# Second layer of a two-layer decoder: own scores on four row strips, one set of eight PSUM banks in turn, and a new table of times

## The chip, the core and the metric

The kernel runs on one core of a Trainium2 chip. The metric is device time in microseconds (us) of one execution: the kernel before has a median of 1911.66 us over three runs (1910.52, 1911.66, 1919.04). One execution was also taken with the hardware profiler; its own time was 1925.23 us, and all views of the trace are from that one.

Engines: TensorE (PE, with its weight loads shown apart as PEld), VectorE (DVE), ScalarE (ACT), GpSimd (POOL) and SyncE (SP, which issues DMAs). Matrix products land in PSUM, which has eight banks of 2 KB per partition, that is 512 float32 each.

## The reference

64 sequences of 64 tokens with 128 features go through two decoder layers. The change concerns the second one alone:

```python
x = x + _L1_attn_ref(_layernorm(x), ...)                  # causal, 16 heads of 8
x = x + _L1_xattn_ref(_layernorm(x), ctx_1024, mask, ...) # 16 heads of 64, relative bias
x = x + _L1_ffn_ref(_layernorm(x), ...)                   # top 1 of 8 experts
...
def _L1_attn_ref(x, Wq, bq, Wk, bk, Wv, bv, Wo, bo):
    q = split_heads(x @ Wq + bq)      # 16 heads of 8
    k = split_heads(x @ Wk + bk)
    v = split_heads(x @ Wv + bv)
    att = jnp.einsum('bhqd,bhkd->bhqk', q, k) * scale
    att = jnp.where(mask, att, -jnp.inf)
    att = softmax(att)
    y = jnp.einsum('bhqk,bhkd->bhqd', att, v)
    return y @ Wo + bo
```

The heads of the first attention ("own" attention here) are eight features wide. The cross attention has 64 features to a head and takes its keys and values from `ctx_1024`. The third part weighs the product of one expert out of eight by its probability. The first layer (a linear attention with its experts, a cross attention, and a routed network of experts whose rows are written to and gathered from device memory) is left as it is.

## The kernel before

**Tiles and groups.** Two sequences make a tile of 128 tokens on the 128 partitions; four tiles (`TG`) make a group, and there are eight groups (`NG`). `xres[g]` holds a group's activations for the whole kernel.

**Stages.** The program runs the first layer's three parts one after another, each with its own division of the PSUM banks, and then the second layer as one stage in which all eight groups are in flight, each some way behind the one before. In the trace the second layer's first matmul stands at about 1305 us and the end at 1923.5.

**PSUM.** `psum_pool` (line 135) fixes how many banks each tag has; `psum` (141) hands out the next bank of a tag. In the second layer the line is

```python
psum_pool(pc, "psC", mm=2, sc=2, tp=1, av=2, py=1)     # 1221
```

Projections, biases and logits (`aq`, `ak`, `av`, `apo`, `xqT`, `xkT`, `xv`, `el`, `eb` by the trace's names) take "mm", some of the own queries and keys "sc"; own scores `asc` and cross scores `xsc` take both "sc" banks; every transpose (`pt_...`) and the experts' choice `oht` the one "tp" bank; the sums of the cross attention `xav` and the experts' products `ey` the two "av" banks; the own sums `apy` and the cross output `xz` the one "py" bank. A tile of a tag waits until all readers of the tile that had the bank before are done.

**Pieces and order.** The work of a group is cut into pieces, each a small function that issues a few instructions on several engines:

- `fetch` (two indirect gathers on GpSimd of the first layer's routed rows), `combine` (their weighted addition on VectorE, with the sums of the norm), `norm_root`, `norm_shift`, `norm_rows`, `by_feature` (four transposes and a copy);
- `attn_queries`, `attn_keys`, `attn_masked`, `attn_v`, then for each of four values `attn_scores`, `attn_exp`, two `attn_keys_first` (transposes) and `attn_sums`, then `attn_out_features`, `attn_out`; `attn_keys` and `attn_masked` write the keys into `kx`, which is one buffer, with zeros where another head's features stand, so that 32 rows of keys serve four heads of eight;
- `cross_load` (SyncE loads the group's context), `project`, `cross_v`, and for each of the four tiles `cross_scores`, `cross_exp`, `cross_whole`, two `cross_keys`, `cross_sums`, `cross_out`;
- `ffn_sums`, `ffn_logits`, `ffn_choice`, `ffn_shares`, `ffn_bias`, and `ffn_experts` with `ffn_add` for each tile and each half of the experts (four additions of 128x128 per call on VectorE). The last one stores the group.

A table (from line 1636) gives each piece a time. `at` collects the pieces, `run_todo` issues them sorted by time, and `keep_in_program_order` keeps each engine to that order: the table is the queue of every engine. Times of the first two parts of the table are relative to a group (`when + 4 * g`), so one unit is a quarter of a group's period; the pieces of the first groups and of the last have rows of their own, with absolute times.

**The own scores.** `attn_scores(s, j)` is called four times for a group. Call `j = (ip, rp)` takes two tiles of tokens (`2*ip + i2`) and half of the heads: two of the four strips of 32 rows of TensorE's array (`2*rp + r`). Each strip has a bank for itself, `[P, 2, 4, S]`, filled for two tiles `i2` and both sequences `b` of a tile:

```python
mm(psc[r][S * b : S * b + S, i2],
   lhsT=s.aq[rs, n * S : (n + 1) * S],        # 32 rows x 64 columns
   rhs=s.kx[rs, :, n * S : (n + 1) * S], ...) # 32 x 256
```

Eight such matmuls make a call. `soft_shift` then adds the causal mask `caus` to each bank in one VectorE instruction over 128x512 (result `p_a`, six buffers of the tag "p" shared with `p_x`), and `soft_max` takes the maximum on VectorE and subtracts it on GpSimd. `attn_exp` works on ScalarE, `attn_keys_first` transposes with TensorE and copies with ScalarE, and `attn_sums` multiplies with the values `vz` (16 small matmuls), takes reciprocals of the sums and multiplies by them into `ay`.

Since `mm`, `transpose` and the engines' methods are wrapped, all instructions of the second layer appear in the trace under the wrapper's line: L64 for matmuls and weight loads, L67 for transposes, L80 for VectorE, ScalarE and GpSimd. They are told apart by the names of their tiles.

## Time and profile before

| | us |
|---|---|
| median of three runs | 1911.66 |
| the profiled execution | 1925.23 |
| its span in the trace | 1923.5 |
| TensorE busy in the span | 1833.8 |
| VectorE busy | 1224.6 |
| ScalarE busy | 959.2 |
| GpSimd busy | 586.4 |
| mean granted clock of TensorE | 0.976 |

The span goes from the first to the last recorded instruction. Busy is the time in which an engine had an instruction in work, without register, branch and DMA-issuing instructions. The profile's page cuts the span into 40 slices of 48 us; the rows for TensorE, VectorE and the clock read as tenths:

```profile
PE   8999999997999999999999998998999999999998
...
DVE  5566666636675766666556754554587687676678
...
PEclk9799999998999999999999998998899999999999
```

The second layer begins in the 28th digit. In the views by instruction, a row has the line, the engine, the operation, the result and its sources by their names in the program, their shapes and the number; then the busy time in all and the mean in nanoseconds of one; then the time that the engine was idle just before such instructions and what released it. In the table of waits a row names who waited, on what, and then the sum, the number and the longest wait in us. In the timeline a row has the start and the length of a run of equal instructions.

### The profile page before, as it was taken

How to read it: one execution, taken by the hardware profiler on the slowest of the kernel's cores; microseconds unless marked ns; L12 is line 12 of the kernel's file. 1: busy time of each engine (PE TensorE's matmuls, PEld its weight loads, DVE VectorE, ACT ScalarE, POOL GpSimd, SP SyncE). 2: the span in 40 equal slices, each digit the busy share in tenths (PEclk: the TensorE clock that was granted, in tenths of full speed). 3: DMA queues.
4: the chain of work that ended last, by engine and by line, in shares of the span. 5: the costliest groups of instructions: out<-in, count | busy, mean ns of one | idle time of the engine just before them, and what ended most of it. 6: DMA issues, size and time to landing. Idle time of an engine off the chain costs nothing.

```text
span 1923.5 us, 42409 instructions
## 1 busy us (share of the span) xinstructions
PE 1833.8 (95%) x17390; PEld 1378.1 (72%) x17390; DVE 1224.6 (64%) x3492; ACT 959.2 (50%) x1743; POOL 586.4 (30%) x600
## 2 busy tenths in 40 slices
PE   8999999997999999999999998998999999999998
PEld 6666667676877777777878775774777776777775
DVE  5566666636675766666556754554587687676678
ACT  2444444444554454445454432335577666666553
POOL 1111111102234242423223231006575554543332
PEclk9799999998999999999999998998899999999999
DMA  8000000000000000000000002321000100100000
GB/s 284 16 2 2 1 2 2 2 1 17 7 6 12 6 12 9 9 12 6 6 2 4 1 3 83 109 62 33 20 13 13 18 16 16 17 9 8 8 2 18
DMA packets 39791, 41.67 MB, mean 22 GB/s; under 512 B 4501, under 2 KB 31445, under 8 KB 39340
## 3 DMA queue, kind: packets, MB, share of 16 engines
q1 hardware_dynamic: 29100, 27.40, 4.6%
q0 software_dynamic: 4096, 6.83, 1.6%
q10 hardware_dynamic: 6400, 4.72, 0.8%
q8 instruction: 137, 2.24, 0.5%
q14 instruction: 58, 0.48, 0.1%
HBM read 28.97 MB, written 11.53 MB: 21 GB/s over the span
## 4 chain that ended last, share of the span: by engine, by line
PE 78%; DVE 11%; issue 4%; POOL 2%; ACT 2%; DMA 1%; ACTq 0%; SPq 0%; POOLq 0%; DVEq 0%
PE sc L64 6%; PE pz L64 6%; PE pu L64 5%; PE xq L64 5%; PE down L64 5%; PE ph L64 5%; PE py L64 3%; PE xqT L64 3%; PE pt_p L67 2%; DVE x L80 2%; PE xz L64 2%; PE sp L64 2%; PE ey L64 2%; PE gg_s L64 2%; PE gu_s L64 2%
## 5 line engine op out<-in xcount | busy, mean ns | idle before, releaser
L983 POOL TENSOR_TENSOR p<-p,rc 128x512 f32<-128x512 f32 x128 | 133.2, 1044 | 297.2 <-DVE rc L982 100.2
L64 PEld LDWEIGHTS down<-w2T,hid 128*128 128x128 f32 x1024 | 129.5, 191 | 44.9 <-DVE x L80 21.6
L960 ACT COPY qx<-xq 128x512 f32<-128x512 f32 x128 | 74.6, 583 | 159.1 <-PE xq L64 158.7
L80 ACT ACTIVATE hid<-ph,wa 128x512 f32<-128x512 f32 x128 | 85.7, 686 | 135.3 <-PE ph L64 135.0
L64 PE MATMUL down<-w2T,hid 128*128 128x128 f32 x1024 | 139.7, 279 | 2.5 <-DVE x L80 2.0
L64 PE MATMUL pu<-pT,kvN 128*128 128x512 f32 x256 | 131.8, 598 | 6.3 <-ACT pT L990 6.2
L64 PE MATMUL sc<-kvT,qx 128*128 128x128 f32 x1024 | 136.4, 276 | 0.0
L64 PE MATMUL ph<-hT,w1T 128*128 128x512 f32 x256 | 133.1, 618 | 0.1
L64 PE MATMUL xq<-kvT,wqk 128*128 128x256 f32 x512 | 132.6, 384 | 0.6
L64 PEld LDWEIGHTS sc<-kvT,qx 128*128 128x128 f32 x1024 | 125.4, 192 | 4.5 <-issue 2.6
L64 PEld LDWEIGHTS pz<-wvo,uT 128*128 128x128 f32 x1024 | 118.4, 192 | 9.1 <-issue 6.2
L64 PEld LDWEIGHTS xq<-kvT,wqk 128*128 128x128 f32 x512 | 93.4, 193 | 37.0 <-issue 25.8
L64 PE MATMUL pz<-wvo,uT 128*128 128x128 f32 x1024 | 119.5, 275 | 0.0
L976 DVE TENSOR_REDUCE nmx<-sc 128x4 f32<-128x512 f32 x128 | 88.0, 687 | 48.9 <-PE sc L64 47.9
L1323 POOL DMA_INDIRECT yk<-y_dram,gidx x64 | 65.3, 1021 | 150.6 <-DMA y_dram<-ye 134.3
L990 ACT COPY pT<-pt_p 128x512 f32<-128x512 f32 x128 | 74.2, 580 | 69.5 <-PE pt_p L67 68.7
L979 ACT ACTIVATE p<-p 128x512 f32<-128x512 f32 x128 | 80.7, 631 | 45.8 <-DVE p L978 33.9
L1097 POOL DMA_INDIRECT xg_dram<-xf,sidx x64 | 63.7, 995 | 121.0 <-DVE si L1090 47.5
L80 POOL TENSOR_TENSOR p_x<-p_x,nmx_x 128x512 f32<-128x512 f32 x64 | 65.4, 1043 | 99.9 <-DVE nmx_x L80 96.9
L80 DVE SCALAR_TENSOR_TENSOR x<-ey,oh_e,x 128x128 f32<-128x128 f32 x256 | 88.8, 348 | 9.4 <-PE ey L64 2.1
L1017 DVE TENSOR_TENSOR x<-pz,x 128x128 f32<-128x128 f32 x32 | 9.3, 292 | 132.8 <-PE pz L64 132.8
L981 DVE TENSOR_REDUCE rc<-p 128x4 f32<-128x512 f32 x128 | 87.0, 680 | 8.7 <-ACT p L979 6.4
(327 smaller groups left out, 4255.0 us busy)
## 6 DMA issues: line engine op xcount, KB each, us to landing
xg_dram<-zero SPq DMA_DIRECT2D x10, 256.0 KB, 7.1
xe<-xg_dram SPq DMA_DIRECT2D x8, 320.0 KB, 3.7
y_dram<-ye ACTq DMA_DIRECT2D x8, 320.0 KB, 3.8
x<-in_x SPq DMA_DIRECT2D x8, 256.0 KB, 12.1
cg<-in_ctx SPq DMA_DIRECT2D x8, 256.0 KB, 2.8
rg<-in_rg SPq DMA_DIRECT2D x8, 256.0 KB, 2.8
rd<-in_rd SPq DMA_DIRECT2D x8, 256.0 KB, 3.2
ru<-in_ru ACTq DMA_DIRECT2D x8, 256.0 KB, 2.7
```

The lines of the kernel that those rows point to most:

```text
L64: return in_order(nc.tensor.matmul(*args, **kwargs))
L67: return in_order(nc.tensor.transpose(*args))
L80: return lambda *args, **kwargs: in_order(getattr(self.engine, name)(*args, **kwargs))
L960: nc.scalar.copy(s.qx[hg][:, :, h : h + 2, :].rearrange("p b h q -> p h b q"), pq)
L976: nc.vector.tensor_reduce(out=nmx, in_=psc, axis=AX, op=ALU.max, negate=True)
L979: nc.scalar.activation(pr, pr, AF.Exp, scale=0.125)
L981: nc.vector.tensor_reduce(out=rc, in_=pr, axis=AX, op=ALU.add)
L983: nc.gpsimd.tensor_tensor(out=pr, in0=pr, in1=bcast(rc, P), op=ALU.mult)
L990: nc.scalar.copy(s.pT[hf], pt)
L1017: nc.vector.tensor_tensor(out=xt, in0=pz, in1=xt, op=ALU.add)
L1097: nc.gpsimd.indirect_dma_start(out=xg_dram[:, :], out_offset=bass.IndirectOffsetOnAxis(ap=sidx[:, TG * s.g + i, k : k + 1], axis=0), in_=s ...
L1323: nc.gpsimd.indirect_dma_start(out=yk, out_offset=None, in_=y_dram[:, :], in_offset=bass.IndirectOffsetOnAxis(ap=gidx[:, TG * s.g + i, k : ...
```

## The change

**Banks.** The second layer's five tags become one, "bank", with eight banks that are handed out in turn: the ninth tile in the program's order takes the bank of the first, whatever both are. All `psum("mm" ...)`, `"sc"`, `"tp"`, `"av"` and `"py"` of the stage become `psum("bank" ...)`, and `attn_queries` and `attn_keys` lose the argument that named their tag.

**Own scores.** `attn_scores(s, i)` is still called four times for a group; call `i` now takes one tile of tokens `i` with both of its sequences and all four strips of 32 rows, each strip with its own bank `[P, 4, S]` (half of a bank is filled). The number of matmuls and their shapes stay: eight of 32x64 weights and 256 columns. The mask is added in four instructions over 128x256, two into each `p` tile. `attn_sums(s, i)` takes both `p` tiles of the call, again with 16 matmuls, and ends in one product over 128x128 where there were two over 128x64. Per call the numbers of instructions on TensorE, ScalarE, GpSimd and SyncE stay; VectorE has one more.

**Times.** Every row of the table has a new time. Part of the group's own-attention rows, and of the start:

```diff
-        psum_pool(pc, "psC", mm=2, sc=2, tp=1, av=2, py=1)
+        psum_pool(pc, "psC", turns=True, bank=8)
...
-        caus = mid(cst[:, C_CAUS : C_CAUS + S], 8)
+        caus = mid(cst[:, C_CAUS : C_CAUS + S], 4)
...
     def transpose4(src, nm):
-        pt = psum("tp" if "tp" in banks else "mm", [P, TG, P], f"pt_{nm}")[:, 0:n]
+        pt = psum(next(t for t in ("tp", "bank", "mm") if t in banks), [P, TG, P], f"pt_{nm}")[:, 0:n]
...
-        def attn_scores(s, j):
-            ip, rp = j // 2, j % 2
-            psc = [psum("sc", [P, 2, 4, S], f"asc_{s.g}_{ip}_{rp}_{r}") for r in range(2)]
-            for i2 in range(2):
+        def attn_scores(s, i):
+            psc = [psum("bank", [P, 4, S], f"asc_{s.g}_{i}_{r}") for r in range(4)]
+            for b in range(2):
+                n = 2 * i + b
+                for r in range(4):
+                    rs = slice(32 * r, 32 * r + 32)
+                    mm(
+                        psc[r][S * b : S * b + S],
+                        lhsT=s.aq[rs, n * S : (n + 1) * S],
+                        rhs=s.kx[rs, :, n * S : (n + 1) * S],
...
-            for r in range(2):
-                s.apr[j, r] = soft_shift(
...
+            for rp in range(2):
+                pr = wk.tile([P, 8, S], F32, tag="p", name=f"p_a{s.g}_{i}_{rp}", bufs=6)
+                for r in range(2):
+                    V.tensor_tensor(out=pr[:, 4 * r : 4 * r + 4, :], in0=psc[2 * rp + r], in1=caus, op=ALU.add)
+                s.apr[i, rp] = pr
...
-            py = psum("py", [P, 2, 4, 2, 9], f"apy_{s.g}_{j}")
+            py = psum("bank", [P, 8, 2, 9], f"apy_{s.g}_{i}")
...
-            (-11.4, 5, 7, fetch, 0),
+            (-12.88, 5, 7, fetch, 0),
...
-            (-10.71, 4, 7, combine, 1),
+            (-10.47, 4, 7, combine, 1),
...
-            (-7.7, 3, 7, cross_load),
+            (-7.1, 3, 7, cross_load),
...
-            (-5.45, 3, 7, attn_scores, 0),
-            (-5.09, 3, 7, attn_v),
-            (-5.06, 3, 7, attn_scores, 1),
+            (-6.14, 3, 7, attn_scores, 0),
+            (-5.84, 3, 7, attn_v),
+            (-4.7, 3, 7, attn_scores, 1),
...
-            (-3.94, 2, 7, attn_scores, 2),
+            (-3.91, 2, 7, attn_scores, 2),
...
-            (0.24, 1, 6, cross_scores, 0),
+            (0.18, 1, 6, cross_scores, 0),
...
-            (1.14, 1, 6, cross_sums, 0),
+            (2.49, 1, 6, cross_sums, 0),
...
-            (6.28, 0, 5, ffn_experts, 0, 0),
-            (6.46, 0, 5, ffn_experts, 0, 1),
-            (6.52, 0, 5, ffn_add, 0, 0),
+            (5.98, 0, 5, ffn_experts, 0, 0),
+            (6.04, 0, 5, ffn_experts, 0, 1),
+            (6.19, 0, 5, ffn_add, 0, 0),
```

The pieces themselves, other than the two shown, do the same work as before. The absolute rows of the start now run from 1.444 to 4.58 (before: 1.046 to 5.455), those of the end from 25.005 to 28.11 (before: 25.8 to 27.638).

## The prediction

> **What bounds the kernel now.** I read the page's totals first, then the windows of the second layer (from 1305 us on, the only part that the diff touches), then who TensorE waited for there, and last the timelines of single calls.

> ```profile
> PE 1833.8 (95%) x17390; PEld 1378.1 (72%) x17390; DVE 1224.6 (64%) x3492; ACT 959.2 (50%) x1743; POOL 586.4 (30%) x600
> ```
> ```profile
> 1305.00:1400.00 95.00, 81.49 (x856) 55.96 (x856) 50.38 (x133) 54.25 (x101) 58.44 (x62) 0.84 0.10 27
> 1400.00:1900.00 500.00, 487.05 (x7132) 364.48 (x7122) 368.99 (x1013) 318.29 (x610) 241.25 (x236) 1.00 0.06 12
> 1900.00:1923.50 23.50, 15.96 (x115) 7.98 (x114) 17.49 (x74) 3.38 (x11) 0.55 (x1) 0.86 0.08 23
> ```
> Columns: the stretch, then busy us of PE, PEld, DVE, ACT, POOL, then the granted clock. TensorE is the bound: in the 500 us in the middle it is idle for 12.9 us, while VectorE is busy for 74%, ScalarE for 64%, GpSimd for 48%. So an instruction less on TensorE is worth its time there, and work on VectorE is hidden while its queue is not late. In the first 95 us TensorE is idle for 13.5 us and its clock is 0.84, which costs about 0.16 x 95 = 15 us more.

> ```profile
> PE xav L64 <- DVE x L80: 7.5, 6, 1.4
> PE apy L64 <- DVE ay L80: 2.5, 2, 1.4
> PE xkT L64 <- DVE x L80: 1.6, 6, 0.3
> PE apy L64 <- DVE x L80: 1.4, 3, 0.5
> PE xkT L64 <- ACT v L80: 1.3, 1, 1.3
> PE ey L64 <- DVE x L80: 1.3, 2, 0.9
> PE pt_a L67 <- ACT pT_a L80: 1.1, 1, 1.1
> ```
> These are waits of TensorE for a PSUM bank: each names the reader of the tile that had the bank before (xav and ey share two "av" banks, apy and xz one "py" bank, all transposes one "tp" bank). They are 16.7 us; four smaller ones of the same sort (0.7, 0.7, 0.7, 0.4) make it 19.2 of the 29.3 us of waits in that table.

> **Part 1: own scores on four strips.** One call is 8 matmuls, two rows each in the trace:
> ```profile
> 1510.31 1.09 PE L64 MATMUL asc<-kx,aqT 32*64 32x256 f32 x16
> 1511.33 1.11 PE L64 MATMUL apy<-vz,pT_a 128*64 128x18 f32 x32
> ...
> 239.51 0.69 PE L64 MATMUL sc<-qxa,phi 32*64 32x128 f32 x32
> 240.14 1.05 PE L64 MATMUL down<-w2T,hid 128*128 128x128 f32 x7
> ```
> The first pair is the call on two strips: 1.02 us to the start of the next piece. The second pair is the first layer's scores, which already run on four strips with the same 32 rows by 64 columns of weights: 32 x 128 = 4,096 columns streamed, as many as 16 x 256 here, in 0.63 us. There are 32 calls (8 groups x 4), and the change keeps that number and that of their matmuls. So 32 x (1.02 - 0.63) = 12.5 us go, a little more at half clock: I take -13. Bounds: 0 if the four strips brought nothing, -14 if all were like the fastest.

> **Part 2: more instructions on VectorE.** 64 additions over 128x512 at 685 ns become 128 over 128x256; the first layer has that shape:
> ```profile
> L80 DVE SCALAR_TENSOR_TENSOR x<-ey,oh_e,x 128x128 f32<-128x128 f32 x256 | 88.8, 348 | 9.4 <-PE ey L64 2.1
> L80 DVE TENSOR_TENSOR p_a<-asc,cst 128x512 f32<-128x512 f32 x64 | 41.1, 685 | 22.4 <-PE asc L64 22.2
> L80 DVE TENSOR_TENSOR ay<-apy,arc 128x64 f32<-128x64 f32 x64 | 11.4, 220 | 1.1
> L80 DVE TENSOR_TENSOR sT<-sc,upto 128x256 f32<-128x256 f32 x128 | 45.4, 417 | 14.6 <-PE sc L64 14.5
> ```
> 128 x 417 - 64 x 685 ns = +9.5 us. The 64 products ay of 220 ns become 32 over 128x128, bounded by 220 and 440 ns; the 348 ns of an operation on that shape is near, so 11.1 against 14.1 us, -3. Together +6.5 us on an engine with 131 us idle in the middle: hidden. On a path it shows as latency: the call's scores are read 4 x 0.42 = 1.67 us after the start of the adds, not 1.37. In the first two groups, where TensorE waits for softmax (2.5 us in all for p_a), I take +1; bounds 0 and 8 calls x 0.3 = +2.4.

> [...]

> **Part 3: eight banks in turn.** A tile now waits for the reader of the tile eight before, whatever its kind. I laid each matmul group's undisturbed time from the timelines along TensorE's order in both programs, and took the TensorE work between the last matmul into a bank and the next tile in it. Under 1.05 us it is 85 times of 732 before and 3 of 796 after; under 2 us 211 and 28. The tile before xav in its bank was an expert product whose four additions (4 x 0.35 = 1.4 us) came late:
> ```profile
> 1592.13 0.33 PE L64 MATMUL xav<-pT_x,v 64*64 64x64 f32 x2
> 1593.88 1.16 PE L64 MATMUL xav<-pT_x,v 64*64 64x64 f32 x62 [1.43 <-DVE x L80]
> ```
> At best all 19.2 us go. New short distances: in each of six groups own-score call 2 is followed by two transposes (0.94) and a cross-scores call (1.09), then xav takes the first of its banks, 2.03 us later. Its additions begin 0.1 us after the scores where VectorE is free and, in the trace's first call of a group, 1.30 us after: 1.30 + 1.67 = 2.97, so up to 0.94 us x 6 = 5.6 us come back. Taken at their word the two give -13.6. I take half, -7, since TensorE freed of one wait runs into the next producer sooner: own scores have 9.6 us of TensorE work before their transposes (median) where they had 14.2, cross scores 19 where they had 13. Bounds -19 and +6.

> **Part 4: the new table.** It moves every piece, GpSimd's gathers and SyncE's context loads among them. Gathers were issued ahead of their addition by 0.57 to 1.53 units of time and now by 0.72 to 1.81; a unit is a quarter of a group's period, some 18 us, so the shortest lead is 13 us where it was 10, and the context load (2.8 us to landing) still stands some 4 units ahead of use. Ten gathers of 1.0 us still precede the first norm on GpSimd, so the first transpose stays near 1323 us; ahead of it TensorE has 11.2 us of work, not 12.9: at worst 1.7 us more idle, of which I take +1. The masked keys' buffer is free before the next group's keys in both.

> The clock is the term that I can't place:
> ```profile
> 1340.00:1350.00 10.00, 8.89 (x66) 5.65 (x64) 5.37 (x11) 5.50 (x12) 7.50 (x8) 0.50 0.00 0
> ```
> Two waits of 1.29 and 1.11 us lie just before this half-clock stretch, which costs 5 us; one stretch more or fewer in the start is +-5, two are +-10. [...] Here waits of little over 1 us sufficed in the start, though not in the middle (1.43 us at clock 1.00). [...]

> **The sum.** -13 + 1 - 7 + 1 = -18 us. The profiled execution took 1925.23 us (its span 1923.5), 13.6 above the median 1911.66; set on the median: **1894 us**.

> **Rivals.** (a) *Every bank wait goes and none comes back:* -13 - 19 = -32, 1880 us. For it the 85 against 3; against it that VectorE's and ScalarE's queues are in order.
> (b) *The waits move:* the new leads cost as much as the old banks (part 3 at +6) and the start loses one clock stretch: -13 + 6 + 5 = -2, 1910 us, no difference that can be told: 0.5% (9.6 us) is about what this kernel's measurement can tell. For it, the shorter distance from own scores to transposes.
> (c) *Four banks held at once:* every own-score call takes half of PSUM until VectorE has read it, and head-of-line TensorE stops at the turn's next tile. If in six groups such a wait of 1.3 us is followed by a half-clock stretch worth 3.4 or more, 6 x 4.7 = +28, less the 13: +15, 1927 us, slower. It decides from 0.9 us of wait per own-score call (29 us in 32). Against it: the middle took 1.43 us waits at full clock.
> (d) *The strips don't overlap more:* -5, 1907 us. The first layer's 0.63 us speaks against it.

> **Chances.** Forecast 0.46 (own range 1884 to 1902), (a) 0.15, (b) 0.21, (c) 0.15, (d) 0.03. Faster by over 0.5% (under 1902): 0.61; within: 0.24; slower: 0.15. The range 1880 to 1917 leaves out (c) and the low part of (a).

> **What would show it.** Part 1: own scores on four strips with about 0.6 us to the next piece. Part 2: 128 additions near 417 ns. Part 3: no xav behind an expert's addition, bank waits in the wait table well under 19 us. Part 4: mean clock from 1305 to 1400 us near 0.84. I am wrong if TensorE's idle time in the middle rises above 13 us with the additions to p_a as releaser, or if the clock in the middle falls below 1.00.

## The result, and the profile after

| | before | changed |
|---|---|---|
| median, us | 1911.58 (4 runs, 1910.52 to 1919.04) | 1892.38 (4 runs, 1889.45 to 1894.31) |
| ratio, with its 95% interval | | 0.9882 (0.9859 to 0.9904) |
| profiled execution, us | 1925.23 | 1893.49 |

The change makes the kernel 19.2 us faster by the medians. The two profiled executions stand 31.7 us apart, and not all of that is the change: in the first trace of before the second layer's first matmul stands at 1305.1 us, in the changed kernel's at 1295.9, and a second trace of before, taken later, has 1297.6. From the second layer's first matmul to the end of the span the three take 618.3, 595.8 and 618.7 us. So between the first two 22.5 us are gone from the part that was changed, and the other 9 are the first stages of one execution.

First the page's totals of the changed kernel, then the windows of its second layer (the stretch; busy us of PE, PEld, DVE, ACT, POOL; granted clock; DMA):

```profile
PE 1807.2 (96%) x17390; PEld 1366.1 (72%) x17390; DVE 1227.3 (65%) x3524; ACT 958.6 (51%) x1743; POOL 587.6 (31%) x600
```
```profile
1305.00:1400.00 95.00, 82.32 (x1180) 59.20 (x1179) 65.84 (x183) 66.32 (x123) 73.81 (x77) 0.89 0.09 25
1400.00:1850.00 450.00, 440.54 (x6628) 336.12 (x6626) 340.97 (x942) 294.89 (x564) 221.19 (x217) 0.99 0.06 12
1850.00:1891.70 41.70, 31.74 (x244) 18.75 (x244) 31.95 (x126) 9.31 (x25) 2.70 (x4) 0.87 0.07 20
```

TensorE is still the bound. The first window is not quite the same piece of the program, since the second layer began 9 us sooner here; its clock is 0.89 where it was 0.84. In the middle it is as busy as before, but its clock, 1.00 before, is 0.99.

The groups that the change touched, and xav, the sums of the cross attention, for which the prediction feared a short way to its bank:

```profile
L80 DVE TENSOR_TENSOR p_a<-asc,cst 128x256 f32<-128x256 f32 x128 | 45.2, 415 | 17.8 <-PE asc L64 17.7
L64 PE MATMUL xav<-pT_x,v 64*64 64x64 f32 x2048 | 37.3, 222 | 0.0
L80 DVE TENSOR_TENSOR ay<-apy,arc 128x128 f32<-128x128 f32 x32 | 9.3, 291 | 1.1
```

The additions are there at 415 ns, and xav waits for nothing at all (7.5 us before). The four additions of a call overlap in the timeline, so together they take 1.41 us; before, the two of a call took 1.29 (at 1511.45). And own scores on four strips have 0.62 us to the next piece, here the values of the cross attention:

```profile
1492.75 1.41 DVE L80 TENSOR_TENSOR p_a<-asc,cst 128x256 f32<-128x256 f32 x4
```
```profile
1349.81 0.69 PE L64 MATMUL asc<-kx,aqT 32*64 32x256 f32 x16
1350.43 1.98 PE L64 MATMUL xv<-xwv,cT 128*128 128x512 f32 x4
```

TensorE's waits in the second layer:

```profile
PE pt_a L67 <- ACT h_a L80: 9.1, 2, 8.3
PE ak L64 <- DVE x L80: 4.5, 3, 1.5
PE pt_e L67 <- ACT h_e L80: 2.3, 2, 1.4
PE pt_pa L67 <- DVE x L80: 1.6, 3, 0.6
PE apy L64 <- ACT pT_a L80: 1.2, 2, 1.0
PE apy L64 <- DVE x L80: 1.1, 3, 0.4
PE apy L64 <- DVE nmr_e L80: 0.7, 2, 0.4
```

Waits for a bank (ak, pt_pa and apy behind x and nmr_e, and 0.2 in a smaller row) come to 8.1 us where they were 19.2. The largest wait is one for data, the first transposes in the start, and a new bank wait stands under it: the own keys, three times 1.5 us. The timeline shows the first of the three, TensorE and then VectorE:

```profile
1490.79 0.69 PE L64 MATMUL asc<-kx,aqT 32*64 32x256 f32 x16
1492.98 1.10 PE L64 MATMUL ak<-hT_a,wl 128*128 128x512 f32 x2 [1.51 <-DVE x L80]
1494.01 1.13 PE L64 MATMUL apy<-vz,pT_a 128*64 128x18 f32 x32
```
```profile
1488.52 2.37 DVE L80 SCALAR_TENSOR_TENSOR x<-yk,wtop,x 128x128 f32<-128x128 f32 x2
1490.93 0.29 DVE L80 BATCH_NORM_STATS2 st_a<-x 128x6 f32<-128x128 f32 x1
1491.26 0.18 DVE L80 BATCH_NORM_AGGREGATE mv_a<-st_a 128x2 f32<-128x6 f32 x1
1491.36 1.48 DVE L80 SCALAR_TENSOR_TENSOR x<-ey,oh_e,x 128x128 f32<-128x128 f32 x4
```

Between an expert product (ey) and the own keys (ak) TensorE's order has one set of transposes, two projections' banks and the four banks of own scores, seven in all: ak takes the expert product's bank. Its four additions stand on VectorE behind the two additions of a tile's gathered rows, which take 2.37 us together here, so the bank comes free at 1492.8. What follows the wait costs as much as the wait: in the next stretch, 3.41 us long, the clock is 0.50 where it was 1.00, which is worth 1.7 us (an estimate: half of the stretch).

```profile
1491.56:1494.97 3.41, 1.99 (x34) 1.26 (x34) 3.30 (x10) 0.85 (x2) 1.07 (x2) 1.00 0.31 43
1494.97:1498.38 3.41, 3.41 (x13) 1.98 (x10) 1.92 (x7) 2.22 (x4) 3.19 (x3) 0.50 0.00 0
```

### The profile page after: what moved, and what is told of

Its sections match the earlier page's. It is cut to its first block, busy times and chain, and to the rows that moved or that the text cites. A ratio compares the mean times of both kernels' runs of the same rounds, so it can differ in the third digit from the quotient of the medians.

```text
span 1891.7 us, 42578 instructions
## 1 busy us (share of the span) xinstructions
PE 1807.2 (96%) x17390; PEld 1366.1 (72%) x17390; DVE 1227.3 (65%) x3524; ACT 958.6 (51%) x1743; POOL 587.6 (31%) x600
## 3 DMA queue, kind: packets, MB, share of 16 engines
q0 software_dynamic: 4096, 6.83, 1.6%
## 4 chain that ended last, share of the span: by engine, by line
PE 78%; DVE 11%; issue 4%; POOL 2%; ACT 2%; DMA 1%; ACTq 0%; SPq 0%; POOLq 0%; DVEq 0%
PE sc L64 6%; PE pz L64 6%; PE pu L64 5%; PE xq L64 5%; PE down L64 5%; PE ph L64 5%; PE py L64 3%; DVE x L80 3%; PE xz L64 3%; PE xv L64 3%; PE pt_p L67 3%; PE ey L64 2%; PE sp L64 2%; PE gg_s L64 2%; PE gu_s L64 2%
## 5 line engine op out<-in xcount | busy, mean ns | idle before, releaser
L64 PEld LDWEIGHTS down<-w2T,hid 128*128 128x128 f32 x1024 | 129.5, 191 | 44.8 <-DVE x L80 21.6
L80 ACT ACTIVATE hid<-ph,wa 128x512 f32<-128x512 f32 x128 | 85.7, 686 | 135.2 <-PE ph L64 134.8
L64 PE MATMUL down<-w2T,hid 128*128 128x128 f32 x1024 | 139.7, 279 | 2.5 <-DVE x L80 2.0
L64 PE MATMUL pu<-pT,kvN 128*128 128x512 f32 x256 | 131.8, 598 | 6.3 <-ACT pT L990 6.2
L64 PE MATMUL sc<-kvT,qx 128*128 128x128 f32 x1024 | 136.3, 276 | 0.0
L64 PE MATMUL ph<-hT,w1T 128*128 128x512 f32 x256 | 133.1, 618 | 0.1
L64 PE MATMUL xq<-kvT,wqk 128*128 128x256 f32 x512 | 132.6, 384 | 0.6 <-ACT qx L960 0.3
L64 PEld LDWEIGHTS sc<-kvT,qx 128*128 128x128 f32 x1024 | 125.4, 192 | 4.5 <-issue 2.6
L64 PEld LDWEIGHTS pz<-wvo,uT 128*128 128x128 f32 x1024 | 118.4, 192 | 9.1 <-issue 6.2
L64 PEld LDWEIGHTS xq<-kvT,wqk 128*128 128x128 f32 x512 | 93.3, 193 | 37.1 <-issue 25.8
L64 PE MATMUL pz<-wvo,uT 128*128 128x128 f32 x1024 | 119.5, 275 | 0.0
L80 DVE SCALAR_TENSOR_TENSOR x<-ey,oh_e,x 128x128 f32<-128x128 f32 x256 | 88.5, 347 | 16.9 <-PE ey L64 8.8
L80 POOL TENSOR_TENSOR p_a<-p_a,nmx_a 128x512 f32<-128x512 f32 x64 | 65.4, 1044 | 89.3 <-PE xsc L64 37.3
```

Source lines behind the costliest of these rows:

```text
L64: return in_order(nc.tensor.matmul(*args, **kwargs))
L80: return lambda *args, **kwargs: in_order(getattr(self.engine, name)(*args, **kwargs))
```

## The experiments

The kernels were measured in sets of one to four, each set beside before, whose median lay between 1910.1 and 1917.3 us from one set to the next. So kernels of different sets are compared by their ratio to before.

| kernel | median, us | ratio to before |
|---|---|---|
| changed (first measurement) | 1892.4 | 0.9882 (0.9859 to 0.9904) |
| changed, own scores as before | 1897.6 | 0.9910 (0.9886 to 0.9934) |
| before, eight banks in turn | 1936.0 | 1.0107 (1.0084 to 1.0130) |
| before, eight banks and four strips | 1951.1 | 1.0182 (1.0159 to 1.0205) |
| changed, expert's additions first | 1889.3 | 0.9863 (0.9840 to 0.9886) |
| before, new table | 2052.6 | 1.0721 (1.0671 to 1.0771) |
| changed again | 1892.8 | 0.9897 (0.9867 to 0.9927) |
| changed, mask added in halves | 1895.9 | 0.9906 (0.9874 to 0.9937) |
| expert's additions first, start filled | 1881.5 | 0.9836 (0.9805 to 0.9867) |
| the same again | 1889.5 | 0.9849 (0.9826 to 0.9871) |
| the same, more moved | 1888.7 | 0.9850 (0.9832 to 0.9869) |
| changed, dense work behind the wait | 1889.2 | 0.9852 (0.9804 to 0.9900) |

**The strips taken back.** `attn_scores` and `attn_sums` of before, with "bank" for their tags, in the changed kernel.

```diff
-        def attn_scores(s, i):
-            psc = [psum("bank", [P, 4, S], f"asc_{s.g}_{i}_{r}") for r in range(4)]
+        def attn_scores(s, j):
+            ip, rp = j // 2, j % 2
+            psc = [psum("bank", [P, 2, 4, S], f"asc_{s.g}_{ip}_{rp}_{r}") for r in range(2)]
...
```

> The changed kernel with the own scores and own sums of before (two strips into two banks per call, mask added in one 128x512 instruction), everything else as changed: eight banks in turn, new table. Theory of the prediction (part 1): each of the 32 calls takes 1.02 instead of 0.63 us of TensorE, so +12.5 us on the changed kernel's 1892.4: 1905 (own scores to the next piece about 1.02 us again). Rival (the strips don't bring it, the gain is table and banks): within 4 us of 1892.4. Rival (four banks held at once are what makes the new waits): the wait of the own keys for a bank, 4.5 us in all in the changed kernel, goes too, so only +4 to +8: 1896 to 1900.

Measured 1897.6: 5.2 us slower than the changed kernel, not 12.5. The two were measured in different sets, and the intervals of their ratios overlap. The window of the middle, with a clock of 1.00, and the longest waits:

```profile
1400.00:1850.00 450.00, 444.45 (x6654) 340.73 (x6651) 336.43 (x923) 294.35 (x567) 222.26 (x217) 1.00 0.06 12
```
```profile
PE pt_a L67 <- ACT h_a L80: 10.6, 3, 8.1
PE pt_pa L67 <- DVE x L80: 3.1, 3, 1.0
PE pt_e L67 <- ACT h_e L80: 2.3, 2, 1.4
```

The own keys' wait is not among the waits. The rival that reckoned with it gave 1896 to 1900, and has it: four banks to a call bring the expert product's bank round two tiles sooner, and by these medians that gives back more than half of the 12.5 us that were reckoned for the strips.

**Eight banks with the old table.** The bank change alone, with four times of the old table moved:

```diff
-            (9.02, 0, 4, ffn_add, 2, 1),
+            (8.83, 0, 4, ffn_add, 2, 1),
-            (6.19, 0, 5, ffn_choice),
+            (5.99, 0, 5, ffn_choice),
-            (1.123, 1, attn_masked, (2,)),
+            (1.1151, 1, attn_masked, (2,)),
-            (27.579, (7, 0), ffn_choice),
+            (27.5645, (7, 0), ffn_choice),
```

> The kernel before with the eight banks in turn alone: own scores on two strips and the old table, in which four pieces are moved a little, since a bank's reader must stand before the eighth tile after it (the addition of expert product 2,1 from 9.02 to 8.83, the experts' choice from 6.19 to 5.99, one piece of the start and one of the end). Theory of the prediction (part 3): -7 us, 1904.6; at best all 19.2 us of bank waits go: 1892. Rival (waits move and a wait in the wrong place halves the clock): 1908 to 1915, with bank waits of other tiles in the wait table.

Measured 1936.0, slower by 20.6 us than before on the same chip. Of its waits in the second layer:

```profile
PE el L64 <- DVE x L80: 6.6, 3, 2.2
PE pt_px L67 <- DVE x L80: 5.3, 5, 1.1
PE xqT L64 <- DVE nmr_a L80: 3.9, 4, 1.0
PE xv L64 <- DVE x L80: 3.4, 1, 3.4
```

The xav waits are gone as reckoned, and others have come, most of them behind VectorE's additions to x: with turns, any piece may follow a bank whose reader stands late in VectorE's queue, logits, transposes and projections among them. The clock from 1400 to 1850 us is 0.98. The theory and the rival were both too hopeful.

**Eight banks and four strips with the old table.** All of the change but its table, with the same four times moved.

> As the kernel before with eight banks in turn and the same four moved pieces, and the own scores on four strips as well: all of the change but its table of times. Theory of the prediction: -13 against the run with eight banks alone, and -20 against before: 1892; the new table then brings nothing (+1 for its start). Rival (the table is made for four banks per call, and the old one pays for it in waits): 1900 or more, that is a table worth 8 us or more.

Measured 1951.1: 15.1 us more than without the strips, where the prediction had 13 less.

```profile
PE xsc L64 <- DVE x L80: 11.2, 5, 2.2
PE pt_a L67 <- ACT h_a L80: 6.6, 1, 6.6
PE el L64 <- DVE x L80: 6.6, 3, 2.2
PE asc L64 <- DVE x L80: 6.5, 5, 1.3
```

The scores have their 0.6 us a call here too, and both kinds of scores, which take four banks and two at a time, now wait 17.7 us for VectorE's additions. From 1400 to 1850 us the clock is 0.96. The rival holds, far beyond its 8 us: with banks and strips given, the table is worth some 57 us (by the ratios, 1.0182 - 0.9882 of 1911.6).

**The new table with the old banks.** The kernel before with the new table, five rows of the last group's end in another order:

```diff
-            (28.098, (7, 3), ffn_experts, 0, 1),
-            (28.099, (7, 2), ffn_experts, 0, 0),
-            (28.1, (7, 3), ffn_experts, 0, 0),
+            (28.0982, (7, 2), ffn_experts, 0, 0),
+            (28.1061, (7, 3), ffn_experts, 0, 0),
+            (28.1081, (7, 3), ffn_experts, 0, 1),
...
```

> The kernel before with the new table alone: own scores on two strips, the five kinds of banks of before; five rows of the last group's end stand in another order, since with two banks for the expert products they would wait for each other for ever. Prediction's term (part 4, the table by itself): +1, about 1916 beside this chip's 1915 for before. Theory after the first four runs (banks and table belong together: the old table with eight banks cost 20 us more, so the new table with fixed banks should pay too): 1925 to 1950, with long bank waits in the wait table. Rival (the new table is the better one whatever the banks are): 1905 or less.

Measured 2052.6, 142.5 us more than before beside it. TensorE waits now for the one transposes' bank (pt_px 12.6 us behind yT and 11.3 behind pT_x) and for the projections' two (xkT 9.8 us behind v). The theory of a table that belongs to its banks had the sign and at most a quarter of the size (1925 to 1950 was expected).

**The expert's additions ahead of the gathered row's.** One time in the changed kernel:

```diff
-            (8.96, 0, 4, ffn_add, 2, 1),
+            (8.92, 0, 4, ffn_add, 2, 1),
```

> The changed kernel with one time moved: the additions of expert product 2,1 from 8.96 to 8.92, so that on VectorE they stand ahead of the first gathered row's addition (2.4 us there) and not behind it. In the profile of the changed kernel TensorE waits 3 times 1.5 us for them when the own keys take that bank, and 2 us later the clock is 0.5 for 3.41 us. Theory (wait and half clock are one cost): the 3 waits of 4.5 us go, and 3 half-clock stretches of 3.41 us, worth 1.7 us each: -9.6, 1883. Rival (the half clock comes from something else): -4.5, 1888. Rival (the wait moves to the next tile or to the gathered rows' addition): within 2 us of 1892.4.

Measured 1889.3. The own keys' three waits and the three half-clock stretches behind them are gone, and the middle is at full clock:

```profile
1400.00:1850.00 450.00, 442.82 (x6682) 337.97 (x6680) 342.98 (x961) 298.06 (x573) 226.50 (x221) 1.00 0.06 12
```

Piece by piece against the trace of the changed kernel, 6.7 us are won between the pieces before the first and behind the last of the three places, and 3.4 lost in the start. By the medians it is 3.1 us, and the intervals overlap: that the waits and the half clock behind them go together is shown in the trace, the 9.6 us of the expectation are not. Against the kernel with two strips in the same set it is 8.3 us (1888.2 to 1892.0 against 1893.4 to 1901.4), which is what the strips bring once that wait is gone.

**The changed kernel again.**

> The changed kernel again, unaltered, for its time beside the others and a second trace. 1892.4 within 3 us. If the half-clock stretches follow what TensorE does in a fixed grid of 3.41 us, the three behind the own keys' wait are in this trace again unless the grid falls otherwise on the waits, and the start's stretches may differ by one (3.4 us).

Measured 1892.8, and its profiled execution took 1887.4 where the first took 1893.5. The three waits are there, 4.5 us in all, but only the first two are followed by half clock; the third is not:

```profile
1632.72:1636.13 3.41, 2.33 (x35) 1.57 (x36) 3.34 (x10) 1.20 (x2) 1.33 (x2) 1.00 0.31 43
1636.13:1639.54 3.41, 3.41 (x15) 2.25 (x15) 2.63 (x9) 3.41 (x7) 2.86 (x3) 1.00 0.00 0
```

The start has one half-clock run of 10.2 us where the first trace had 10.2, 3.4 and 6.8 us. In all the second layer stands at half clock for 24 us where it stood for 42, and to the end of the span it takes 588.0 us, 7.9 less; half of the difference in half clock is 9. So two executions of one program stand 6 to 8 us apart with the same three waits in both, and by the traces they differ in how much half clock stood behind such places.

**More work on VectorE.** Each addition of the mask cut into two halves:

```diff
-                    V.tensor_tensor(out=pr[:, 4 * r : 4 * r + 4, :], in0=psc[2 * rp + r], in1=caus, op=ALU.add)
+                    for h in range(2):
+                        V.tensor_tensor(out=pr[:, 4 * r + 2 * h : 4 * r + 2 * h + 2, :],
+                                        in0=psc[2 * rp + r][:, 2 * h : 2 * h + 2, :], in1=caus, op=ALU.add)
```

> The changed kernel with each of the four additions of the mask in an own-score call cut into two over 128x128: 256 in place of 128. By the row of 128x128 additions from PSUM (292 ns) eight take 2.34 us and not 1.67, so +0.67 us a call, +21 us of VectorE's busy time in all. Prediction's part 2 (VectorE's work is hidden): within 4 us of the changed kernel. Rival (the four banks' release is on the path, so the additions' latency shows in every call): 0.67 x 32 = +21 us. Between (only where a bank comes round soon, as at the own keys): 3 x 0.67 and half-clock stretches, +2 to +8.

Measured 1895.9 beside 1892.8 for the changed kernel, the runs of the two overlapping. The trace shows that less was added than planned: the halves overlap too, and VectorE is busy with them for 53.3 us where it was for 45.2.

```profile
L80 DVE TENSOR_TENSOR p_a<-asc,cst 128x128 f32<-128x128 f32 x256 | 53.3, 279 | 17.0 <-PE asc L64 17.0
```

So the rival's price is 8 us here and not 21, and the 3 us of the medians do not settle it alone. But no wait of TensorE in this trace names an addition to p_a: as far as it shows, VectorE's work on the scores is hidden.

**The start filled.** The previous swap, and four pieces of group 0 moved ahead of the first transposes (at 1.467):

```diff
-            (1.521, 0, cross_v, 2, 0),
+            (1.4661, 0, cross_v, 2, 0),
-            (1.531, 0, cross_v, 2, 1),
+            (1.4662, 0, cross_v, 2, 1),
-            (1.532, 0, cross_v, 0, 0),
+            (1.4663, 0, cross_v, 0, 0),
-            (1.528, 0, project, "kT", 2),
+            (1.4664, 0, project, "kT", 2),
```

> The run with the additions of expert product 2,1 moved, and in the start four pieces of group 0 that need only the context (cross values 2,0, 2,1 and 0,0 and key projection 2) moved ahead of the first transposes, where TensorE is idle for 8.6 us. They are 3 x 0.86 + 1.73 = 4.3 us of TensorE. Theory (idle time filled, and the work gone from where it stood): -4.3 us and perhaps a half-clock stretch less, 1.7: 1883 to 1886 beside 1889 for the run without. Rival (they were themselves fillers between other waits, which open again): within 1.5 us of 1889.

Measured 1881.5, 11.3 us less than the changed kernel in the same set, with no overlap of their runs (1879.6 to 1883.5 against 1887.4 to 1893.4). It is under the 1883 to 1886 of the expectation. The wait before the first transposes is 4.1 us where it was 8.3. The same kernel in a later set:

> The run with the start filled again, for the comparison on one chip: 1881.5 within 3 us.

Measured 1889.5 with before at 1917.3: by the ratio 0.9849 after 0.9836. It missed its 3 us. In its trace the second layer takes 6.8 us more than in the first one's (584.4 against 577.5 us from its first matmul to its last), spread over many places, with a few waits of xsc and xav that the trace puts down to nothing but issue (1.5 us in all). Both ratios lie under both of the changed kernel (0.9882 and 0.9897), by 0.33 to 0.61%, some 6 to 12 us; the intervals of the later measurement overlap, the runs of the earlier one do not.

**Still more moved.** Three further pieces into the start, and four in the end of the last group ahead of transposes for which TensorE waits.

```diff
-            (3.365, 1, project, "kT", 3),
+            (1.4665, 1, project, "kT", 3),
...
-            (28.044, (6, 0), ffn_experts, 0, 0),
+            (28.0415, (6, 0), ffn_experts, 0, 0),
...
```

> The run with the start filled, and three further pieces moved into the 4.1 us that TensorE still waits before the first transposes (key projection 3 of group 1, cross values 0,0 and 0,1 of group 1: 1.73 + 2 x 0.86 = 3.45 us), and in the last group's end four pieces moved ahead of transposes for which TensorE waits 1.4 and 0.9 us. Theory: -3.4 - 1.7 = -5 on the run with the start filled. Rival (the pieces were fillers where they stood, or the end is set by the last group's chain on ScalarE and VectorE and not by TensorE): within 1.5 us of it.

Measured 1888.7 beside 1889.5: no gain that can be told. The rival holds, and the trace shows both places. The wait before the first transposes is gone, but cross values ahead of them now wait for their bank (xv behind v, 3.1 us), and in the end a cross output does (xz behind x, 2.2 us).

**Before again, for its trace.**

> The kernel before again, unaltered, for a second trace: the profiled execution of before was 13.6 us over the median, and its second layer began at 1305 us where the eight other traces have 1295 to 1298. If that was one execution's first stages, the second layer begins near 1296 here and lasts 614 us as in the first trace, or some half-clock stretches of 1.7 us less or more.

Measured 1918.1, and the second layer begins at 1297.6 and ends its matmuls 614.2 us later, 613.9 in the first trace. The late start was that execution's.

**Dense work behind the wait.** To tell whether the idle time itself halves the clock, one time of the changed kernel was moved so that an expert product follows the own keys and the own sums come after it:

```diff
-            (-2.89, 2, 7, attn_sums, 2),
+            (-2.79, 2, 7, attn_sums, 2),
```

> The changed kernel with one time moved: own sums 2 from -2.89 to -2.79, so that behind the own keys, which wait 1.5 us three times, TensorE has an expert product (128x128 weights, 512 columns) next and the own sums (128x64 weights, 18 columns) after it, and not the other way round. The wait itself stays. In the traces so far the clock of each 3.41 us of a fixed grid follows the work of the 3.41 us before it: columns streamed times the share of the array in use, 1,277 to 1,480 in the three places that were followed by half clock, 1,510 in the one that was not, 4,096 when full. Theory (work in the grid's stretch decides, not the idle time): the stretch with the wait now holds some 2,050, so no half clock at the three places with the three waits unchanged at 4.5 us; -5.1 us, 1887. Rival (the idle time decides): half clock at two or three of them as before, 1892.

The waits, then the stretch with the first of them and the next one, then those with the third:

```profile
PE ak L64 <- DVE x L80: 4.5, 3, 1.5
```
```profile
1493.48:1496.89 3.41, 2.20 (x15) 0.99 (x16) 3.34 (x9) 1.07 (x2) 1.28 (x2) 1.00 0.42 38
1496.89:1500.31 3.42, 3.42 (x41) 2.76 (x38) 2.60 (x8) 3.42 (x7) 2.99 (x3) 1.00 0.02 5
```
```profile
1633.43:1636.84 3.41, 1.91 (x20) 0.87 (x20) 3.23 (x11) 0.83 (x2) 1.86 (x2) 1.00 0.23 30
1636.84:1640.25 3.41, 3.41 (x42) 2.12 (x41) 2.62 (x8) 3.36 (x6) 2.58 (x3) 1.00 0.08 13
```

The waits are the same 4.5 us, and none of the three is followed by half clock, though at the third place TensorE is busy for only 1.91 us of its stretch, less than the 1.99 of the stretch in the changed kernel that was. So in this trace the idle time alone did not decide. What the moved expert product did is shown at the first place alone: its stretch holds the product whole, with a sum (columns times the share of the array, as in the expectation) of 2,115, and with the own sums there instead the sum would be about 1,310 (an estimate: 1,024 of the own keys and 288 of the own sums). At the second and third place the grid falls so that the stretch ends before the product or 0.15 us into it; there it is the projections and scores ahead of the wait that keep the sum at 2,028 and 1,801. Measured 1889.2; the interval of its ratio is too wide to tell 5 us.

## Why the prediction came out right, and where its steps were wrong

The time was forecast at 1894 and measured at 1892.4. The sum was right; two of its four terms, the banks and the table, were not, if each is taken as what its part does by itself. So that the forecast came within 2 us is in part luck: what the start won stands in no term, and by the traces the changed part lost more than the medians say.

The 22.5 us that the second layer lost between the first two traces close as follows (between the later traces of the two kernels it is 30.7). With each piece's undisturbed time laid along TensorE's order, as the prediction did, the pieces' sum fell by 13.4 us (542.9 to 529.5; an estimate that moves by about 1 us with what is taken as undisturbed); what TensorE took beyond it fell by 7.3 us in the first 95 us (32.1 to 24.8), by 2.1 in the middle (31.7 to 29.6) and by 2.0 in the last 20 us (6.1 to 4.1); behind the last matmul 3.2 were added, and the last piece makes up the rest. That the middle gained so little has two reasons in the traces: its bank waits fell only from 11.9 to 8.1 us, since the rest of the 19.2 stood in the start (6.1) and in the end (1.3), and half clock took 5.1 back.

| term of the sum | predicted | in the traces of the whole change | the part by itself |
|---|---|---|---|
| 1, four strips | -13 (0 to -14) | -13.4 of TensorE's work | -5.2 under the new table, -8.3 without the own keys' wait, +15.1 under the old |
| 2, VectorE | +1 (0 to +2.4) | 415 and 291 ns, hidden | +3 for twice the additions, the runs overlapping |
| 3, eight banks | -7 (-19 to +6) | -11.1 of bank waits (6.1 of them in the start), +5.1 of half clock | +20.6 under the old table |
| 4, new table | +1 | the start -7.3 and -11.1 in two traces (the 6.1 of row 3 within it), the end +3.2 and -2.0 | some -57 given 1 and 3, +142.5 without them |

*Part 1.* A call takes 0.62 us to the next piece after it in the trace, and the pieces' undisturbed times sum to 529.5 us where they were 542.9. The first layer's row was the right one to price it by. That the gain reaches the end was assumed, and was true for the call's work only: the four banks brought a new wait.

*Part 2.* The additions' mean was as forecast, 415 ns for 417. The latency was not: the means were added up, but the four overlap, and a call takes 1.41 us and not 1.67, against 1.29 and not 1.37 before. Under the new table no wait of TensorE names an addition to p_a; under the old one the scores wait 17.7 us for VectorE, though it was not the scores' own additions but the experts' that were late.

*Part 3* took half of what was possible, and the whole change gave about that: 19.2 us of bank waits fell to 8.1, and four half-clock stretches in place of one between 1400 us and the end of the middle (3 x 1.7 us more) took 5.1 back. The short way from own scores to xav cost nothing. The reckoned list had only distances in TensorE's work, and those under 2 us; the wait that came, at the own keys, has 2.9 us of TensorE's work before it (transposes, projections and scores, 1488.53 to 1491.4 in the timeline), and came because the reader stood behind 2.4 us of another piece in VectorE's queue.

*Part 4* is the step that failed: "at worst 1.7 us more idle, of which I take +1". The idle time before the first transposes grew by 5.5 us, from 2.8 to 8.3. Two runs divide this growth; here are before, the new table with the old banks, and the eight banks with the old table:

```profile
PE pt_a L67 <- issue: 2.8, 1, 2.8
```
```profile
PE pt_a L67 <- ACT h_a L80: 4.7, 1, 4.7
```
```profile
PE pt_a L67 <- ACT h_a L80: 7.1, 1, 7.1
```

The table by itself brought 1.9 us, near the worst that the prediction allowed it. The larger part comes with the banks, for which the prediction had no such term: the first gather on GpSimd starts 3.3 us after the first layer's last store is issued in the three traces with the old tags (1305.12 to 1308.41 in that of before), and 4.8 to 5.4 us after it in all eleven traces with eight banks (1295.84 to 1300.80 in that of the changed kernel). Why it does is not shown.

And the start as a whole, 95 us from the second layer's first matmul, went the other way: it lost 24.8 us against undisturbed pieces, and 21.0 in the second trace, where it had lost 32.1. Its 6.1 us of bank waits went, and it stood at half clock for 20.5 us and not 30.7; so what came behind the first wait, and the clock, which the prediction had named as the term that it could not place, outweighed that wait. Its row for the clock was misread, too: the half clock began at 1340.0, so that of the two waits put "just before" it the one of 1.11 us (1340.6 to 1341.7) lies inside it.

Last, the table is not a term of its own. The prediction priced it only at its start, while the same banks and strips under the old order cost 36 us more than before, and the new order under the old banks 142. The terms 1 and 3 were reckoned along the new order; that this is why the sum held is argued, not shown.

*The rivals.* (c), the wait followed by half clock, happened, three times for 1.5 + 1.7 us, at the own keys and not at the scores' readers; with 9.6 us of cost it stayed under the 29 that it needed. The 3.4 us that it set for the half clock is what a stretch of 6.8 us costs by the estimate above, and the trace of before has three of these in the start; at the own keys each stretch was 3.41 us long. What the prediction put down as a sign of its being wrong, a clock under 1.00 in the middle, came true without making it wrong. (b), the waits that move, is the course of the run with the old table.

The end of the span is the one place that got worse: after the last matmul VectorE has three tiles' additions left where it had one, so the end comes 7.6 us after that matmul and not 4.4. From the two traces, before first:

```profile
1919.05 1.51 DVE L80 SCALAR_TENSOR_TENSOR x<-ey,oh_e,x 128x128 f32<-128x128 f32 x4 [0.49 <-PE ey L64]
```
```profile
1884.33 4.46 DVE L80 SCALAR_TENSOR_TENSOR x<-ey,oh_e,x 128x128 f32<-128x128 f32 x12
```

What stays open: how the 57 us of the table divide among its 435 rows, why the gathers start later with eight banks, and why one and the same program took 6.8 us more in one execution than in another without a longer wait for data or banks.

## What to carry to other kernels

When a diff changes how buffers are handed out and also the order of the work, price the two as one: here the cost of a bank came from where its reader stood in the reader's queue (2.4 us of another piece ahead of it, three waits of 1.5 us), so look for the late reader, not only for the short distance. Where banks go round in turn, a piece that takes four at once shortens every other piece's distance, and one row of the order (an addition moved ahead of a slower one) can give back what it costs (here the three waits, 4.5 us in all). And look at what stands around a wait on TensorE: behind the same wait of 1.5 us the clock stayed at 1.00 six times, where the work of its 3.41 us (columns times the share of the array) came to 1,489 to 2,115, and was 0.50 six times, where it came to 1,277 to 1,479.

## What the runs showed of the hardware that was not expected

```profile
1664.22:1667.63 3.41, 1.98 (x68) 1.45 (x67) 1.96 (x6) 1.55 (x5) 2.04 (x2) 1.00 0.02 5
1667.63:1671.04 3.41, 3.41 (x41) 2.21 (x41) 0.89 (x5) 2.99 (x6) 0.00 (x0) 1.00 0.00 0
```

The changed kernel's wait of 1.5 us at the own keys, with the own sums behind it, stands nine times in three traces (its own two and that with the mask added in halves). Six times half clock followed, with sums of 1,277 to 1,479, and three times it did not, with 1,489, 1,510 and 1,599: the same work and the same wait, and the grid lay otherwise on them. And half clock followed without any idle time, too: in the run with the dense work TensorE has no gap from 1783.60 to 1787.01, but logits and own sums, with 8 and 18 columns, fill most of that stretch (a sum of 1,401), and the next is at half clock.

```profile
1783.60:1787.01 3.41, 3.41 (x50) 3.05 (x49) 0.91 (x4) 1.52 (x4) 2.02 (x2) 1.00 0.02 5
1787.01:1790.42 3.41, 3.41 (x5) 1.33 (x5) 2.96 (x14) 0.01 (x1) 0.00 (x0) 0.50 0.00 0
```
